# Background matmuls one at a time in a score loop: a bank held over, sums read from PSUM, work moved between VectorE and GpSimd

## The chip, the cores and the metric

The kernel runs on one core of a Trainium2 chip. A core has a matrix engine (TensorE, "PE" in the profile, with its weight loads as "PEld"), a vector engine (VectorE, "DVE"), a scalar engine for activations (ScalarE, "ACT"), a general engine (GpSimd, "POOL") and a queue engine that starts transfers (SyncE, "SP"). The metric is the device time of one execution in microseconds. Three runs before the change gave a median of 6430.78 us, from 6425.47 to 6433.72.

## The reference

The input is x of shape 8 × 128 × 36 × 36. Layer 0 normalises it in groups, applies a 1×1 convolution, and runs a convolutional attention: queries (3×3, 'SAME'), keys and values (3×3, 'VALID') of the input, softmax over 1156 key positions, then two 1×1 convolutions with a tanh between, added to x. Layer 1 takes the 1296 positions as tokens of 128 channels and applies additive attention and a gated expert layer:

```python
t = jnp.tanh(q[:, :, None, :] + k[:, None, :, :])
scores = jnp.einsum('bijd,d->bij', t, w) + bw[0]
attn = jax.nn.softmax(scores, axis=-1)
```

The scores need a tanh for each pair of tokens and each channel: 8 × 1296 × 1296 × 128 of them. The expert layer chooses 8 tokens for each of 64 experts by a softmax over the tokens, pools them, runs a small network per expert and adds its result back to the chosen tokens.

## The kernel before, in words

**The score loop.** The kernel turns the tanh sum into quotients. Each score is a sum of terms n/d, where both n and d are small matrix products over features of the keys (`kf`) and of the queries (`qf`). A *unit* is one batch, one chunk of 432 queries (three per batch) and one tile of 128 keys (ten, and a remainder of 16). A full unit has twelve *slots*, the remainder three. A slot is two halves of products: two matmuls for numerators `n` (PSUM pool `ps_n`, four banks, two taken per slot) and two for denominators `d` (pool `ps_d`, two tiles of two banks). All matmuls are fp32 and appear in the trace as two passes each. By k % 3, two slots in three contract over 32 rows ("fives"), and n of one slot and d of the slot three later stand on different rows, so they can stream together. The third is a slot of "sixes", over 64 rows.

Per slot p the program order is: pending background steps of the other engines (`take_turns`), n of slot p (`numerators`), d of slot p + 3 with its logarithm on ACT, and after every second slot an exponential that turns two logarithms into reciprocals (`denominators`, L815 and L818), the multiplies of slot p (`terms`), and then background matmuls (`matmul_turn`). Each engine takes its instructions in that order.

`terms` has two forms. For k in `DVE_PAIRS` VectorE multiplies in place in the two n banks (L836, L840) and adds them to a running sum (L837, L842), and the banks stay taken until these adds. For the others VectorE multiplies into an SBUF tile `rp` (L846, three buffers) and GpSimd adds it to its own sum (L851, L853). At the end of a unit GpSimd adds the sums (L860, L863), and ACT takes the exponential (L878).

**The background.** Everything else is cut into generators that yield between steps: `normal` (group statistics), `conv_turns` (the convolutions), `layer0`, `tokens` and `keys` for the next batch, `attend` (the weighted sum of tokens for a finished chunk) and `gating`. They stand in four lanes. A step yields whether its next one wants matmuls and how many slots it rests. A turn takes a bank with `aux(...)` from the same four of `ps_n`, so a turn's bank is one less for n; it is read by VectorE or ACT in a later step. A running account (`balance`) is debited with the columns of a turn (`behind`: the columns, at least 128, plus 20 per matmul) and credited with `PACE` per slot; a lane other than the first may begin a turn when it isn't negative.

**What the change touches.** `conv_turns` (L243) does nine taps as pairs: two matmuls into one bank, one VectorE copy or add (L258, L260), and so on. `layer0` (L329) computes, per chunk of queries, exponentials of ten score tiles, their total (L374, GpSimd), value sums in pairs of tiles (L395, L397), the total over partitions and its reciprocal on ACT (L405, L406), and the product with it (L412). `attend` (L601) does, for each of four token tiles of a chunk, eleven matmuls in two turns of six and five, with a VectorE copy (L625) and an add (L628) to join them in SBUF, then reciprocal, multiply-add and statistics (L630 to L636). `tokens` (L536) and `gate_logits` (L680) normalise tiles of 128 channels with GpSimd, about two tiles per step. Before the loop, the image of batch 1 is loaded (L917).

Of the kernel before, what the change touches and what calls it, by code (L numbers as in the profile page):

```python
# [57 lines left out]
DVE_PAIRS = (2, 5, 8, 11)  # L58
PACE = 370
# [5 lines left out]
def kernel(  # L65
# [55 lines left out]
    with ExitStack() as loop, ExitStack() as score:  # L121
# [28 lines left out]
        def aux(name):  # L150
            return ps_n.tile([128, 512], F32, tag="n", name=name)
# [73 lines left out]
        TAKE = (False, 1)  # L225
# [17 lines left out]
        def conv_turns(taps, rows, y0, x0, width, dst):  # L243
            r0, nr = rows
            for t0 in range(0, 9, 2):
                some = TAPS[t0 : t0 + 2]
                ps = aux("pc")[:, : nr * width]
                for t, (dy, dx) in enumerate(some):
                    bmm(
                        ps.rearrange("p (a b) -> p a b", b=width),  # L250
                        taps[:, (t0 + t) * C : (t0 + t + 1) * C],
                        xpad[:, y0 + dy + r0 : y0 + dy + r0 + nr, x0 + dx : x0 + dx + width],
                        start=(t == 0),
                        stop=(t == len(some) - 1),
                    )
                yield TAKE
                if t0 == 0:
                    nc.vector.tensor_copy(dst, ps)  # L258
                else:
                    nc.vector.tensor_add(dst, ps, dst)  # L260
                yield matmuls()
# [67 lines left out]
        def layer0(b):  # L329
# [33 lines left out]
            for c in range(NCH):  # L363
# [22 lines left out]
                ax = chunk_tile("ax0")  # L386
                for j0 in range(0, NDT, 2):
                    pa = aux("pa0")
                    for j in (j0, j0 + 1):
                        n = DTILES[j][1]  # L390
                        bmm(pa[:, :CH], vw[:n, j, :], ex[j][:n], start=(j == j0), stop=(j > j0))
                    yield TAKE
                    if j0 == 0:
                        total(NDT - 1)
                        nc.vector.tensor_scalar(ax, pa[:, :CH], 1.0 / D, None, ALU.mult)  # L395
                    else:
                        nc.vector.scalar_tensor_tensor(  # L397
                            ax, pa[:, :CH], 1.0 / D, ax, ALU.mult, ALU.add
                        )
                    yield matmuls()  # L400
                pt = aux("pt0")
                bmm(pt[:, :CH], ones[:DT], tot[:DT], start=True, stop=True)
                yield TAKE
                ri = chunk_tile("ri0")
                nc.scalar.activation(ri, pt[:, :CH], AF.Ln, scale=1.0 / D)  # L405
                nc.scalar.activation(ri, ri, AF.Exp, scale=-1.0)  # L406
                yield matmuls(1)
# [4 lines left out]
                nc.vector.tensor_mul(ax, ax, ri)  # L412
# [78 lines left out]
        def tokens(b):  # L491
# [44 lines left out]
            for t in range(NKT):  # L536
                n = KT[t][1]
                nc.gpsimd.tensor_scalar(
                    xh[:n, t, :C], tok[:n, t, :], mv[:n, t, 0:1], rs[:n, t : t + 1],
                    ALU.subtract, ALU.mult,  # L540
                )
                if t % 2 == 1:
                    yield step()
# [57 lines left out]
        def attend(b, c, es):  # L601
# [8 lines left out]
            for i in range(TPC):  # L610
                at = c * TPC + i
                nc.sync.dma_start(t2[:T, at, :], tokd[b][at * T : (at + 1) * T])
                sums = two.tile([T, C + 1], F32, tag="sums", name="sums")
                for some in (range(6), range(6, NKT)):
                    pa = aux("pa1")[:T, : C + 1]
                    for j in some:
                        if j < NKT - 1:
                            e, v = es[j][:, i * T : (i + 1) * T], xh[:, j, :]
                        else:
                            rows = slice(32 * i, 32 * i + REM)  # L620
                            e, v = es[j][rows, :T], xr[rows]
                        bmm(pa, e, v, start=(j == some[0]), stop=(j == some[-1]))
                    yield TAKE
                    if j < NKT - 1:
                        nc.vector.tensor_copy(sums, pa)  # L625
                        yield matmuls()
                    else:
                        nc.vector.tensor_add(sums, pa, sums)  # L628
                inv = small.tile([T, 1], F32, tag="inv", name="inv")
                nc.vector.reciprocal(inv, sums[:, C : C + 1])  # L630
                nc.vector.scalar_tensor_tensor(  # L631
                    t2[:T, at, :], sums[:, :C], inv, t2[:T, at, :], ALU.mult, ALU.add
# [16 lines left out]
        def gate_logits(b, chunks):  # L649
# [30 lines left out]
            for j, t in enumerate(tiles):  # L680
                nc.gpsimd.tensor_scalar(  # L681
# [20 lines left out]
        def gate_tokens(b):  # L702
# [41 lines left out]
            for t in range(NT):  # L744
                bmm(pp[:, :E], t2[:T, t, :], gT[t // half][:, t % half, :],
                    start=(t == 0), stop=(t == NT - 1))
            yield TAKE
# [135 lines left out]
        class Lane(deque):  # L883


            wants_matmuls, ready = True, 0

            def run(self, p):
# [4 lines left out]
                self.ready = p + rest  # L893

# [11 lines left out]
        def matmul_turn(p):  # L906
# [3 lines left out]
            for lane in lanes:  # L910
                while lane.due(p, True) and behind[0] == before:
                    if lane is not first_of_all and balance[0] < 0 or lane is gates and urgent:
                        break
                    lane.run(p)
            balance[0] = min(balance[0] - (behind[0] - before) + PACE, PACE)

        load_x(1)  # L917
# [16 lines left out]
        for p, (u, k) in enumerate(slots):  # L934
# [26 lines left out]
            matmul_turn(p)  # L961
# [187 lines left out]
```

## Time and profile before

| what | value |
|---|---|
| median of three runs | 6430.78 us |
| the profiled execution's own time | 6428.41 us |
| its span | 6426.7 us |
| granted TensorE clock, mean | 0.966 |
| first to last L815 (the score loop) | about 199 to 6244 us |
| idle of ACT before L815, waiting for PE's d | 643.3 us in 719 waits |
| idle of POOL before L853, waiting for DVE's rp | 975.3 us in 660 waits |

The page of a profile lists, in this order: the busy time of each engine; the span in 40 slices; transfers; the chain of work that ended last; and the groups of instructions, each as source line, engine, operation, tiles written and read, shapes, count, then busy time and mean in ns, then the idle time just before them and what ended it. A busy TensorE is not a TensorE at its peak, because its matmuls overlap. "n<-qf,kf" means a matmul into a tile n from tiles qf and kf. Other answers of the trace give busy times in a stretch of time, single instructions in order of time, and the waits between engines.

### The profile page before, as it was taken

The numbers are of one execution on the slowest core, as the hardware profiler recorded it, in microseconds if no ns is written. First come the engines' busy times: TensorE is split into PE (matmuls) and PEld (weight loads), VectorE is DVE, ScalarE is ACT, GpSimd is POOL, SyncE is SP. The second block draws the span as 40 slices with busy tenths as digits, with TensorE's granted clock in tenths as the row PEclk, the third lists the DMA queues.
The fourth block names the chain that finished last, engine by engine and source line by source line (L and its number), as shares of the span: only waits on it lengthen the run. The fifth ranks groups of instructions, "written<-read, shape, count | busy, mean of one in ns | idle before, by whom it ended". The sixth has DMA issues, their size and how long they took to land.

```text
span 6426.7 us, 106771 instructions
## 1 busy us (share of the span) xinstructions
PE 6054.8 (94%) x40448; PEld 2813.9 (44%) x40448; DVE 4900.4 (76%) x9315; ACT 5354.6 (83%) x5426; POOL 4798.1 (75%) x2966
## 2 busy tenths in 40 slices
PE   8999999999999999999999999999999999999986
PEld 4444444444444444444444444444444444544432
DVE  3687778877788777888788887887778877778862
ACT  1788898888888888888888888888888888989970
POOL 3677777787777877777787787778777787888870
PEclk9999999999999999999999999999999999999997
DMA  0200011000110002100111001100011000100017
GB/s 28 66 31 23 22 63 36 30 24 27 56 46 19 24 27 68 33 26 22 44 47 38 22 23 53 43 32 25 20 63 43 23 24 27 61 26 28 24 66 253
DMA packets 155284, 265.78 MB, mean 41 GB/s; under 512 B 53712, under 2 KB 79824, under 8 KB 154768
## 3 DMA queue, kind: packets, MB, share of 16 engines
q1 hardware_dynamic: 154768, 258.95, 12.5%
q8 instruction: 318, 5.21, 0.3%
q14 instruction: 198, 1.62, 0.1%
HBM read 196.81 MB, written 61.83 MB: 40 GB/s over the span
## 4 chain that ended last, share of the span: by engine, by line
PE 67%; DVE 12%; ACT 7%; issue 7%; POOL 6%; DMA 1%; SPq 0%; POOLq 0%; DVEq 0%; ACTq 0%
PE n L793 30%; PE d L793 10%; PE pc L237 7%; PE pa L237 6%; ACT lq L815 5%; DVE n L840 3%; DVE rp L846 3%; PE s L237 3%; PE pk L237 3%; PE pq L237 2%; DVE accd L842 2%; POOL accp L853 2%; DVE t L631 1%; PE n L800 1%; POOL t L681 1%
## 5 line engine op out<-in xcount | busy, mean ns | idle before, releaser
L853 POOL TENSOR_TENSOR accp<-accp,rp 128x864 f32<-128x864 f32 x1464 | 2965.2, 2025 | 1028.0 <-DVE rp L846 975.3
L793 PE MATMUL n<-qf,kf 32*128 32x432 f32 (+1 forms) x11520 | 3239.2, 579 | 93.4 <-DVE rp L846 47.0
L815 ACT ACTIVATE lq<-d 128x864 f32<-128x864 f32 x2952 | 2552.6, 882 | 690.7 <-PE d L793 643.3
L793 PE MATMUL d<-qf,kf 32*128 32x432 f32 (+1 forms) x11520 | 2876.6, 568 | 21.2 <-ACT lq L815 16.4
L846 DVE TENSOR_TENSOR rp<-n,lq 128x432 f32<-128x432 f32 x3984 | 2202.6, 600 | 623.7 <-PE d L793 399.3
L818 ACT ACTIVATE lq<-lq 128x1728 f32<-128x1728 f32 x1488 | 2429.0, 1632 | 47.1
L793 PEld LDWEIGHTS n<-qf,kf 32*128 32x128 f32 (+1 forms) x11520 | 1167.1, 187 | 1703.4 <-DVE rp L846 586.3
L793 PEld LDWEIGHTS d<-qf,kf 32*128 32x128 f32 (+1 forms) x11520 | 1038.8, 188 | 392.2 <-issue 254.1
L840 DVE TENSOR_TENSOR n<-n,lq 128x432 f32<-128x432 f32 x1440 | 811.7, 608 | 280.1 <-PE n L793 239.2
L842 DVE TENSOR_TENSOR accd<-n,accd 128x432 f32<-128x432 f32 x1440 | 867.4, 602 | 24.7
L851 POOL TENSOR_TENSOR accp<-rp 128x864 f32<-128x864 f32 x264 | 533.8, 2022 | 221.1 <-DVE rp L846 217.5
L237 PE MATMUL pa<-xh,e 128*108 128x129 f32 x1920 | 262.6, 284 | 55.6 <-DVE rp L846 34.7
L860 POOL TENSOR_TENSOR accp<-accp 128x432 f32<-128x432 f32 x264 | 290.8, 1101 | 16.2
L237 PEld LDWEIGHTS pa<-xh,e 128*108 128x108 f32 x1920 | 223.3, 175 | 179.1 <-DVE rp L846 107.4
L594 POOL TENSOR_SCALAR qf<-qf,cs_s 128x432 f32<-128x432 f32 x192 | 262.7, 1374 | 42.0 <-ACT qf L593 42.0
L863 POOL TENSOR_TENSOR accd<-accp,accd 128x432 f32<-128x432 f32 x240 | 265.6, 1107 | 28.5 <-DVE accd L842 10.4
L237 PE MATMUL s<-q,k 128*116 128x432 f32 x480 | 229.8, 570 | 3.3 <-DVE q L260 2.1
L237 PEld LDWEIGHTS pk<-xT,a_k 128*128 128x128 f32 x1408 | 172.2, 193 | 109.8 <-DVE accd L842 27.6
L374 POOL TENSOR_TENSOR tot<-tot,e 116x432 f32<-116x432 f32 x192 | 212.0, 1104 | 6.1
L835 DVE TENSOR_TENSOR accd<-n,lq 128x432 f32<-128x432 f32 x240 | 144.9, 604 | 91.6 <-PE n L793 60.5
L381 ACT ACTIVATE e<-s 116x432 f32<-116x432 f32 x240 | 125.0, 521 | 106.6 <-PE s L237 105.5
L237 PE MATMUL pk<-xT,a_k 128*128 128x128 f32 (+1 forms) x1408 | 203.2, 288 | 2.6 <-DVE accd L842 2.3
(175 smaller groups left out, 4144.4 us busy)
## 6 DMA issues: line engine op xcount, KB each, us to landing
kf<-kd SPq DMA_DIRECT2D x240, 512.0 KB
kd<-ks SPq DMA_DIRECT2D x160, 256.0 KB
w<-in_weight_dram SPq DMA_DIRECT2D x32, 1024.0 KB
x<-in_x_dram SPq DMA_DIRECT2D x8, 648.0 KB
t<-tokd SPq DMA_DIRECT2D x96, 54.0 KB
t2d<-t2T SPq DMA_DIRECT2D x24, 216.0 KB
res<-t2d SPq DMA_DIRECT2D x8, 648.0 KB
out_dram<-res SPq DMA_DIRECT2D x8, 648.0 KB
```

What stands on the lines that cost most here:

```text
L237: mm(out, lhsT, rhs, **kw)
L594: nc.gpsimd.tensor_scalar(qf[:, 1, :], qf[:, 0, :], cs_s[:, q : q + 1], None, ALU.mult)
L793: mm(outs[h][:, :CH], kf[rows[h], q, :], qf_of[b, c, q][rows[h], part, :], start=True, stop=True)
L815: nc.scalar.activation(lq[:, o : o + 2, :], d[:, :, :CH], AF.Ln)
L818: nc.scalar.activation(some, some, AF.Exp, scale=-1.0)
L840: mult(ns[h], ns[h], lq[:, o + h, :])
L842: nc.vector.tensor_add(live["d"], ns[h], live["d"])
L846: mult(rp[:, h, :], ns[h], lq[:, o + h, :])
L851: nc.gpsimd.tensor_add(live["p"], live["r"], rp)
L853: nc.gpsimd.tensor_add(live["p"], live["p"], rp)
L860: nc.gpsimd.tensor_add(s[:, 0, :], s[:, 0, :], s[:, 1, :])
L863: nc.gpsimd.tensor_add(d, s[:, 0, :], d)
```

## The change

There are five edits.

1. *Turns of one matmul.* A new yield value `HELD` marks a turn after which the bank stays open: the accumulation goes on in the lane's next turn. `conv_turns` yields after every matmul (HELD after the first of a pair), so do the value sums of `layer0`; `attend` puts all eleven matmuls in one bank, in turns of four, four and three; `gate_tokens` splits its twelve in the same way. While a lane holds, only that lane gets turns.
2. *Few turns in slots of sixes.* In a slot with k % 3 == 2 a turn needs a balance of at least `LATE` = 400. `PACE` goes from 370 to 380, and the balance may rise to twice `PACE`.
3. *Sums read from PSUM.* `attend` has no copy or add to SBUF; its reciprocal and multiply-add read the bank. In `layer0` the total and its reciprocal come before the last pair of value sums, whose sum is made in PSUM and multiplied from there; the factors 1/D are gone from both sides of the quotient.
4. *Three slots on VectorE.* `DVE_PAIRS` loses slot 11, which then goes by `rp` and GpSimd.
5. *Normalising shared.* Odd tiles of the two normalising loops go to VectorE. The load of batch 1's image before the loop is gone; `normal` makes it as for the other batches.

```diff
-DVE_PAIRS = (2, 5, 8, 11)
-PACE = 370
+DVE_PAIRS = (2, 5, 8)
+PACE, LATE = 380, 400
...
-        TAKE = (False, 1)
+        TAKE, HELD = (False, 1), (True, 1)
...
-                yield TAKE
+                    yield TAKE if t == len(some) - 1 else HELD
...
+                ri = chunk_tile("ri0")
                 for j0 in range(0, NDT, 2):
-                    pa = aux("pa0")
+                    if j0 == NDT - 2:
+                        pt = aux("pt0")
+                        bmm(pt[:, :CH], ones[:DT], tot[:DT], start=True, stop=True)
+                        yield TAKE
+                        nc.scalar.activation(ri, pt[:, :CH], AF.Ln)
+                        nc.scalar.activation(ri, ri, AF.Exp, scale=-1.0)
+                        yield matmuls()
+                    pa = aux("pa0")[:, :CH]
                     for j in (j0, j0 + 1):
                         n = DTILES[j][1]
-                        bmm(pa[:, :CH], vw[:n, j, :], ex[j][:n], start=(j == j0), stop=(j > j0))
-                    yield TAKE
+                        bmm(pa, vw[:n, j, :], ex[j][:n], start=(j == j0), stop=(j > j0))
+                        yield TAKE if j > j0 else HELD
                     if j0 == 0:
                         total(NDT - 1)
-                        nc.vector.tensor_scalar(ax, pa[:, :CH], 1.0 / D, None, ALU.mult)
+                        nc.vector.tensor_copy(ax, pa)
+                    elif j0 < NDT - 2:
+                        nc.vector.tensor_add(ax, pa, ax)
                     else:
-                        nc.vector.scalar_tensor_tensor(
-                            ax, pa[:, :CH], 1.0 / D, ax, ALU.mult, ALU.add
-                        )
+                        nc.vector.tensor_add(pa, pa, ax)
+                        nc.vector.tensor_mul(ax, pa, ri)
                     yield matmuls()
...
-                nc.gpsimd.tensor_scalar(
+                (nc.gpsimd, nc.vector)[t % 2].tensor_scalar(
...
-                sums = two.tile([T, C + 1], F32, tag="sums", name="sums")
-                for some in (range(6), range(6, NKT)):
-                    pa = aux("pa1")[:T, : C + 1]
...
+                pa = aux("pa1")[:T, : C + 1]
+                for j in range(NKT):
...
+                    bmm(pa, e, v, start=(j == 0), stop=(j == NKT - 1))
+                    if j in (3, 7):
+                        yield HELD
+                yield TAKE
                 inv = small.tile([T, 1], F32, tag="inv", name="inv")
-                nc.vector.reciprocal(inv, sums[:, C : C + 1])
+                nc.vector.reciprocal(inv, pa[:, C : C + 1])
                 nc.vector.scalar_tensor_tensor(
-                    t2[:T, at, :], sums[:, :C], inv, t2[:T, at, :], ALU.mult, ALU.add
+                    t2[:T, at, :], pa[:, :C], inv, t2[:T, at, :], ALU.mult, ALU.add
                 )
...
+                if t in (3, 7):
+                    yield HELD
...
-        def matmul_turn(p):
+        def matmul_turn(p, k):
             before = behind[0]
-            for lane in lanes:
+            least = LATE if k % 3 == 2 else 0
+            for lane in [lane for lane in lanes if lane.holds] or lanes:
                 while lane.due(p, True) and behind[0] == before:
-                    if lane is not first_of_all and balance[0] < 0 or lane is gates and urgent:
+                    if lane is not first_of_all and balance[0] < least or lane is gates and urgent:
                         break
                     lane.run(p)
-            balance[0] = min(balance[0] - (behind[0] - before) + PACE, PACE)
-
-        load_x(1)
+            balance[0] = min(balance[0] - (behind[0] - before) + PACE, 2 * PACE)
```

## The prediction

> **What bounds the kernel now.** I read the page's busy shares first, then the chain that ended last and the costliest groups.
>
> ```profile
> span 6426.7 us, 106771 instructions
> PE 6054.8 (94%) x40448; PEld 2813.9 (44%) x40448; DVE 4900.4 (76%) x9315; ACT 5354.6 (83%) x5426; POOL 4798.1 (75%) x2966
> PE 67%; DVE 12%; ACT 7%; issue 7%; POOL 6%; DMA 1%; SPq 0%; POOLq 0%; DVEq 0%; ACTq 0%
> ...
> L853 POOL TENSOR_TENSOR accp<-accp,rp 128x864 f32<-128x864 f32 x1464 | 2965.2, 2025 | 1028.0 <-DVE rp L846 975.3
> ...
> L815 ACT ACTIVATE lq<-d 128x864 f32<-128x864 f32 x2952 | 2552.6, 882 | 690.7 <-PE d L793 643.3
> L846 DVE TENSOR_TENSOR rp<-n,lq 128x432 f32<-128x432 f32 x3984 | 2202.6, 600 | 623.7 <-PE d L793 399.3
> ```
>
> No engine is full: ACT waits 643 us for denominators from PE, POOL 975 us for products from DVE. TensorE carries the chain but its busy share includes pipeline latency. A unit (12 slots of one key tile) is the right ruler, so I next read the busy times of six single units of batches 4, 5 and 7. The columns are busy us of PE, PEld, DVE, ACT, POOL, then the clock.
>
> ```profile
> 3318.62:3347.20 28.58, 24.87 (x111) 10.92 (x110) 22.73 (x41) 20.42 (x21) 26.09 (x23) 0.82 0.03 5
> 3428.19:3450.39 22.20, 21.90 (x110) 9.76 (x106) 19.57 (x37) 20.31 (x20) 16.58 (x10) 1.00 0.22 78
> 3522.54:3548.09 25.55, 22.77 (x157) 12.96 (x155) 24.30 (x49) 20.29 (x21) 16.34 (x9) 1.00 0.09 25
> 3593.98:3620.07 26.09, 26.06 (x178) 10.11 (x175) 17.98 (x33) 24.49 (x30) 24.07 (x17) 1.00 0.07 21
> 3911.01:3940.48 29.47, 24.43 (x112) 11.22 (x115) 21.35 (x40) 20.31 (x20) 25.85 (x23) 0.77 0.06 19
> 6181.65:6201.59 19.94, 19.23 (x98) 7.68 (x96) 16.73 (x31) 19.75 (x20) 16.33 (x10) 1.00 0.00 1
> ```
>
> The last has no background: 19.94 us, ACT 19.75 of them. That is the floor. The others: gate normalising (28.58, POOL 26.09); a convolution (22.20); attention sums (25.55, DVE 24.30); scores s (26.09, ACT 24.49 and POOL 24.07); token normalising (29.47, POOL 25.85). So what ends a unit differs by its background. Loop time from first to last Ln is 6045 us; less 24 remainder units at about 7 us, 240 full units average 24.5.
>
> Two waits matter. The time-ordered view shows one bank wait: the second n matmul starts only when the first in-place add of the slot before is done (1014.62 + 0.62 = 1015.24), since the transposes hold one of four banks, and the next Ln starts after 1.27 us idle. And it shows VectorE against POOL:
>
> ```profile
> 1013.32 0.59 PE L241 MATMUL tp<-ident,t 108*128 108x108 f32 x4
> 1013.60 1.11 DVE L840 TENSOR_TENSOR n<-n,lq 128x432 f32<-128x432 f32 x2
> ...
> 1014.62 1.24 DVE L842 TENSOR_TENSOR accd<-n,accd 128x432 f32<-128x432 f32 x2
> ...
> 1015.27 0.62 PE L793 MATMUL n<-qf,kf 32*128 32x432 f32 x1 [0.44 <-DVE accd L842]
> ...
> 1016.35 0.89 ACT L815 ACTIVATE lq<-d 128x864 f32<-128x864 f32 x1 [1.27 <-PE d L793]
> ```
>
> ```profile
> 4086.65 3.70 DVE L291 SCALAR_TENSOR_TENSOR dev<-dev,gn_mv 128x1 f32<-128x1 f32 x1
> ```
>
> This DVE instruction has one element per lane and lasts 3.70 us, until POOL's run of operations (four L681, one L853: 4085.23 to 4090.34) is over.
>
> **What the skill says.** "SBUF — State Buffer", Who interferes with whom: VectorE and GpSimd share a port pair under an exclusive lock; a VectorE instruction with two SBUF inputs, or a tensor_scalar in the two-port mode, is shut out for whole GpSimd instructions, one with at most one SBUF input is not. The trace agrees: L631 (two SBUF inputs) has median 674 ns, 350 to 1841; L846 (one from PSUM) is steady at 600. "VectorE: DVE Perf Modes", Mode 2×_2P — use both read ports for one tensor: an fp32 tensor_scalar from SBUF to SBUF takes both ports. L213, such a one of 11 or 12 elements, lasts 0.158 to 1.37 us, which agrees. "TensorE: Matmul & The Clock Gate", What's actually happening: the clock drops when PE has been idle; the two normalising units show 0.82 and 0.77.
>
> **The change part by part**, against the profiled execution (6428.4 us, span 6426.7).
>
> *Sums read PSUM.* Per token tile (96 in all) one copy L625 (0.288) and one add L628 (0.292) go, and L631 loses its second SBUF input: 0.915 mean toward the 0.350 minimum. That is 0.58 + 0.565 = 1.14 us of DVE. An attention unit does about 3 tiles; its L631 are the bad ones (1.664 mean in the unit above), so DVE loses 3 × (0.58 + 1.31) = 5.7 us, and 1.2 more from the slot below: 24.3 falls to 17.4. VectorE no longer bounds it. What is late next is PE: I take the 25.5 down by 1.2 only, because of the held bank (below). Range 0 to 3. There are 44 × 2 passes per chunk against 56 or so in a unit, 1.55 units per chunk, 4.6 per batch: −5.5 us a batch. Dividing by D moved from L395/L397 to nowhere, and L412 (0.816) becomes a PSUM multiply of 0.604 (as L846): 24 × 0.21 = 5 us, off the path. The pt turn goes ahead of the last pa0 turn: its two ACT passes (0.516 + 0.563) now hide under pa0 matmuls. Nothing counted.
>
> *Three slots on VectorE.* Slot 11 moves: per unit DVE loses two adds, 2 × 0.602 = 1.2 us (289 us in all; the multiplies stay), POOL gains one L853, 2.025 us (486 us in all). POOL at 4798 goes to 5284, less the normalising below (11 tiles a batch, about 0.79 each, 8 batches, −70): 5214. Convolution units end on PE with DVE 19.6 close: I give them −0.2 each, 8 a batch: −1.6. Score and query-block units have ACT 24.5 and POOL 24.1; POOL becomes 26.1 of 26.1, the first to fill: +0.3 each (0 to +1), 7 a batch: +2.
>
> *One-matmul turns, bank held.* PE's work is the same: the same matmuls, same banks' sums. A 2-matmul turn put 1.44 us (four passes of 432 columns, which follow each other at 0.36) between a slot and the next; now 0.72. Denominators come more evenly, but a bank is held over most slots instead of some 40% of them (370/904). With it held, the second n waits for the slot before: after a PSUM-multiply slot that is about hidden by n, d and one turn; after an in-place slot, the add ends some 2.7 us after n began (1.0 + 1.1 + 0.6), PE alone needs 1.7, so 1.0 us is exposed unless a turn fills 0.72. Behind that n on PE stand the next d and so ACT's next Ln. Slots of sixes need a balance of 400, so with 380 per slot and 452 per turn a convolution skips about one in six slots, always a six, half of them while held; attention turns (4 × 149 = 596) skip nearly every six while held. Cost: about 0.4 × 1.0 per in-place slot in convolutions, 0.75 × 1.0 in attention, times three. Against it stand the lumps: the ACT idle of 643 us. I take both as cancelling in convolutions and the attention cost as already in the −1.2 above.
>
> *Normalising shared.* Five of eleven L538 and six of twelve L681 per batch move to DVE: POOL loses 11 × 0.79 = 8.7 us in two units with POOL near 26 of 29, where DVE then idles on POOL (4.40 us before one L846), PE behind it. POOL gains 2.0 per unit. On DVE each costs some 0.2 us alone (a 128-element bn_stats takes 0.27) but may wait for POOL, up to the 3.70 above; behind it on DVE stand the slot's multiplies, so the banks, so PE. Net per unit between −5 and +3; I take −2.5, two a batch: −5.
>
> *The rest.* Group load x[1] goes from the start into the loop, where batches 2 to 7 already have it four slots ahead of use: 0. PACE 380 for 370 finishes the background 2.7% sooner: 0 at constant work. In the tail the last chunk's three waiting tiles save 0.58 each and four L681 in a row (3.12) are halved: −3.
>
> Sum: −5.5 − 1.6 + 2 − 5 = −10.1 a batch; times 7.5 (the first batch's preparation lies before the loop, the last has no successor) = −76, with the tail −79. 6428 − 79 = 6349, so 6350 in the runs, whose median 6430.8 lies 2 us over the profiled one.
>
> **Rivals.** (A) Held banks and POOL win: slower. From the point where every in-place slot exposes its 1.0 us while held in 60% of cases, 240 × 3 × 0.6 = +430 us less the lumps' relief of about half the 643 us: +110, with POOL's +2 unchanged and my gains halved (−40): 6500. For it: 535 PE weight loads already wait on L842 for 248 us. Against: many fall in slots that PE fills anyway. Chance 0.27. (B) Nothing moves: PE passes plus their gaps fill about 92% of a unit (22.2 of the convolution's), so smoothing has nothing to win and DVE's relief is slack: 6425. Chance 0.07. (C) Large gain: lumps were the cause of ACT's idling and half of the 643 us returns, plus the sum above less overlaps (−79 + 20): −380, 6050; half as strong, 6240. For: units run at 19.94 when undisturbed. Against: convolution units are only 2.3 over it with ACT's own background work inside. Chance 0.16 for below 6270. My forecast 0.50.
>
> **Numbers.** A measurement tells about 0.2% (13 us) from no change. Faster 0.68 (0.50 + 0.16 + edge of B), same 0.05, slower 0.27. Range 6220 to 6500 holds most of the forecast, B and A's nearer half; the forecast's own is 6290 to 6410.
>
> **What would show it.** Right: attention units near 24 us with L631 at 0.4; L625 and L628 gone; L853 near 1700 instructions; POOL above 80%; normalising units under 27. Wrong: n waiting on L842 well over 248 us with ACT idle above 643, or DVE tensor_scalars of several us.

## The result, and the profile after

The changed kernel took 6549.68 us (median of four runs, 6539.88 to 6552.72) against 6432.25 us for the kernel before on the same chip: a ratio of 1.0182, 95% interval 1.0164 to 1.0199. It is slower by 117 us, and lies 50 us above the upper end of the predicted range.

The page of the changed kernel, with the lines that answer to those shown of before (line numbers are one lower there: L852 was L853, L814 was L815, L845 was L846, L841 was L842):

```profile
span 6549.1 us, 106863 instructions
PE 6230.2 (95%) x40448; PEld 2792.7 (43%) x40448; DVE 4594.4 (70%) x8731; ACT 5372.1 (82%) x5426; POOL 5206.4 (79%) x3118
PE 63%; POOL 15%; issue 8%; DVE 7%; ACT 6%; DMA 1%; SPq 0%; POOLq 0%; ACTq 0%; DVEq 0%
L852 POOL TENSOR_TENSOR accp<-accp,rp 128x864 f32<-128x864 f32 x1704 | 3448.8, 2024 | 961.3 <-DVE rp L845 884.1
L845 DVE TENSOR_TENSOR rp<-n,lq 128x432 f32<-128x432 f32 x4464 | 2488.6, 601 | 1231.8 <-PE d L792 659.3
L814 ACT ACTIVATE lq<-d 128x864 f32<-128x864 f32 x2952 | 2570.7, 883 | 797.6 <-PE d L792 721.0
```

The moves happened as planned: VectorE fell by 306 us (4900.4 to 4594.4), GpSimd rose by 408 (4798.1 to 5206.4). But GpSimd's share of the chain that ended last went from 6% to 15%, and ACT now waits 721 us for denominators, not 643. The list of waits shows what changed. Its columns are the waiting engine and tile, what it waited for, us in total, times, and the longest. First after, then before:

```profile
PEld n L792 <- DVE rp L845: 793.7, 1207, 3.6
PEld pa L238 <- issue: 214.3, 385, 1.2
PEld pc L238 <- issue: 198.6, 389, 1.2
PEld n L792 <- DVE accd L841: 153.7, 269, 2.3
DVE rp L845 <- POOL accp L850: 144.8, 86, 3.2
DVE rp L845 <- POOL accp L852: 76.7, 54, 3.5
```

```profile
PEld n L793 <- DVE accd L842: 248.3, 535, 3.3
DVE rp L846 <- POOL accp L851: 78.1, 32, 8.7
PEld pc L237 <- issue: 66.4, 371, 0.6
PEld pa L237 <- issue: 46.9, 272, 0.2
```

VectorE's products now wait 222 us for GpSimd to free an `rp` tile, 78 before. And the weight loads of background turns stand 413 us at "issue" (waiting for nothing that the profile shows), 113 before. The "issue" time by itself is no measure of a loss: it falls to 244 us in the run below with turns of two, for 32 us of time, and is still 403 us in the run with a fourth buffer, which is 130 us faster. The wait that the slower rival was built on, n for the in-place add, fell from 248 to 154, about as the number of those adds did (L841 x960, from x1440).

Single units of batch 4 show where the time is (columns as before: busy us of PE, PEld, DVE, ACT and POOL with their counts, clock, transfers). The first is unit 0 of chunk 0, then come unit 6 of chunk 0 (a convolution) and units 0 and 1 of chunk 1 (the last does attention sums):

```profile
3308.87:3338.20 29.33, 25.03 (x109) 12.36 (x110) 15.62 (x29) 20.73 (x21) 24.17 (x14) 0.83 0.07 22
3471.02:3495.08 24.06, 23.93 (x123) 9.04 (x119) 18.89 (x36) 20.33 (x20) 18.34 (x10) 1.00 0.06 22
3568.46:3597.24 28.78, 27.31 (x128) 11.81 (x126) 17.57 (x33) 21.06 (x22) 21.88 (x13) 0.88 0.07 22
3597.24:3622.03 24.79, 24.79 (x165) 13.74 (x163) 18.37 (x41) 20.54 (x21) 18.36 (x10) 1.00 0.09 27
```

The first units of chunks took 23.45 and 23.15 us before; now they take 29.33 and 28.78 at a lower clock. Over all 24 chunks the first units, each from its first Ln to the next unit's, take 650.2 us, 557.5 before: 93 of the 125 us that the score loop lost. The attention unit is hardly shorter than its 25.55, although VectorE is down from 24.30 to 18.37. Inside the third of these units, in order of time (start, duration, engine, what; in brackets the idle time before it and what ended it):

```profile
3578.14 1.12 POOL L862 TENSOR_TENSOR accd<-accp,accd 128x432 f32<-128x432 f32 x1
...
3579.21 1.38 POOL L596 TENSOR_SCALAR qf<-qf,cs_s 128x432 f32<-128x432 f32 x1
...
3579.95 1.65 ACT L814 ACTIVATE lq<-d 128x864 f32<-128x864 f32 x2
...
3580.54 2.04 POOL L850 TENSOR_TENSOR accp<-rp 128x864 f32<-128x864 f32 x1
...
3582.62 1.12 DVE L845 TENSOR_TENSOR rp<-n,lq 128x432 f32<-128x432 f32 x2 [2.58 <-POOL accp L850]
...
3583.28 0.96 PE L792 MATMUL n<-qf,kf 64*128 64x432 f32 x1 [1.32 <-DVE rp L845]
...
3586.44 0.89 ACT L814 ACTIVATE lq<-d 128x864 f32<-128x864 f32 x1 [3.16 <-PE d L792]
```

The same core in a stretch just after the stall, with its clock:

```profile
3586.00:3590.00 4.00, 4.00 (x13) 1.39 (x13) 1.49 (x4) 1.07 (x2) 0.77 (x1) 0.50 0.00 0
```

The old unit's slots 9, 10 and 11 all went to GpSimd, its two sums and a feature product follow, so the first add of the new unit starts late. Slots 0 and 1 of the new unit need `rp` tiles too, five slots in a row, and slot 0's tile is only freed by slot 1's add (L850). VectorE's next product has no `rp` tile until that add ends (2.58 us), the banks stay full, PE starts no matmul for some 1.3 us, its granted clock then is 0.50, and ACT is idle for 3.16 us.

### The profile page after: what moved, and what is told of

It reads as the page before. It is cut to its first block, busy times and chain, and to the rows that moved or that the text cites. A ratio compares the mean times of both kernels' runs of the same rounds, so it can differ in the third digit from the quotient of the medians.

```text
span 6549.1 us, 106863 instructions
## 1 busy us (share of the span) xinstructions
PE 6230.2 (95%) x40448; PEld 2792.7 (43%) x40448; DVE 4594.4 (70%) x8731; ACT 5372.1 (82%) x5426; POOL 5206.4 (79%) x3118
## 4 chain that ended last, share of the span: by engine, by line
PE 63%; POOL 15%; issue 8%; DVE 7%; ACT 6%; DMA 1%; SPq 0%; POOLq 0%; ACTq 0%; DVEq 0%
PE n L792 29%; PE d L792 9%; PE pa L238 7%; PE pc L238 7%; POOL accp L852 7%; ACT lq L814 4%; PE s L238 3%; DVE n L839 2%; DVE rp L845 2%; POOL qf L596 2%; POOL accp L850 2%; PE pk L238 2%; DVE accd L841 1%; POOL accp L859 1%; PE d L799 1%
## 5 line engine op out<-in xcount | busy, mean ns | idle before, releaser
L852 POOL TENSOR_TENSOR accp<-accp,rp 128x864 f32<-128x864 f32 x1704 | 3448.8, 2024 | 961.3 <-DVE rp L845 884.1
L792 PE MATMUL n<-qf,kf 32*128 32x432 f32 (+1 forms) x11520 | 3330.7, 583 | 126.3 <-DVE rp L845 93.4
L845 DVE TENSOR_TENSOR rp<-n,lq 128x432 f32<-128x432 f32 x4464 | 2488.6, 601 | 1231.8 <-PE d L792 659.3
L814 ACT ACTIVATE lq<-d 128x864 f32<-128x864 f32 x2952 | 2570.7, 883 | 797.6 <-PE d L792 721.0
L792 PE MATMUL d<-qf,kf 32*128 32x432 f32 (+1 forms) x11520 | 2957.3, 572 | 44.6 <-ACT lq L814 40.7
L839 DVE TENSOR_TENSOR n<-n,lq 128x432 f32<-128x432 f32 x960 | 545.3, 609 | 226.4 <-PE n L792 206.9
L841 DVE TENSOR_TENSOR accd<-n,accd 128x432 f32<-128x432 f32 x960 | 577.7, 602 | 16.4
L850 POOL TENSOR_TENSOR accp<-rp 128x864 f32<-128x864 f32 x264 | 533.6, 2021 | 31.7 <-DVE rp L845 31.4
L238 PEld LDWEIGHTS pa<-xh,e 128*108 128x108 f32 x1920 | 238.8, 182 | 190.8 <-issue 124.5
L238 PE MATMUL pa<-xh,e 128*108 128x129 f32 x1920 | 298.3, 296 | 9.2 <-DVE accd L841 4.6
L238 PE MATMUL pa<-e,vw 116*128 116x432 f32 x480 | 231.2, 571 | 1.3 <-DVE accd L841 0.5
```

The source lines that it names most:

```text
L238: mm(out, lhsT, rhs, **kw)
L792: mm(outs[h][:, :CH], kf[rows[h], q, :], qf_of[b, c, q][rows[h], part, :], start=True, stop=True)
L814: nc.scalar.activation(lq[:, o : o + 2, :], d[:, :, :CH], AF.Ln)
L839: mult(ns[h], ns[h], lq[:, o + h, :])
L841: nc.vector.tensor_add(live["d"], ns[h], live["d"])
L845: mult(rp[:, h, :], ns[h], lq[:, o + h, :])
```

## The experiments

### Slot 11 back on VectorE, longer turns, GpSimd's normalising, the old account

Four runs undo one part each in the changed kernel.

*Slot 11.*

```diff
-DVE_PAIRS = (2, 5, 8)
+DVE_PAIRS = (2, 5, 8, 11)
```

> The kernel after, with slot 11 back on VectorE (four slots in place). POOL theory (GpSimd, with three rp slots in a row at the end of a unit and the sums behind them, makes VectorE wait for rp buffers; those waits are 222 us of the L850 and L852 rows after, 78 and a little before): most of them go and the first units of a chunk fall from 29 toward 24, so 6450 to 6480. Switch theory (each extra change of PE between slot products and a background turn costs about 0.24 us, 520 more of them): slot 11 has no part in it, 6535 to 6555.

Measured: 6454.81 us, 1.0037 of the kernel before (1.0024 to 1.0050). Putting it back alone returns 95 of the 117 us. In the score loop of the two traces 87 of 92 us lie in the first units of chunks (563.1 us, from 650.2). Some of it comes by way of the clock: its mean is 0.964 in the changed kernel and 0.975 here, which is 74 us less of TensorE's time lost to a lower clock (6549 × 0.036 less 6453 × 0.025; an estimate, and the most that the clock can have given). The products' wait for GpSimd is down to this:

```profile
DVE rp L845 <- POOL accp L850: 31.3, 20, 2.4
```

*Turns of two matmuls in convolutions and value sums.*

```diff
-                    yield TAKE if t == len(some) - 1 else HELD
+                yield TAKE
...
-                        yield TAKE if j > j0 else HELD
+                    yield TAKE
```

> The kernel after, with the convolutions' and value sums' matmuls again in turns of two, so without a bank held between their turns (attention and pooling keep theirs). Switch theory: some 51 turns a batch go, 408 in all, at 0.24 us: -98, so 6450, and the small gaps of PE return to those of before. POOL theory: these waits stay, 6530 to 6560.

Measured: 6518.01 us, 1.0135 (1.0118 to 1.0152): 32 us less than the changed kernel, between the two expectations. With slot 11 on VectorE in both kernels the same step is worth 68 us (6454.81 above, 6387.02 below).

*All normalising on GpSimd.*

```diff
-(nc.gpsimd, nc.vector)[t % 2].tensor_scalar(
+nc.gpsimd.tensor_scalar(
```

> The kernel after, with both normalising loops on GpSimd alone. Port theory (VectorE's share waits for GpSimd; 40 xh tiles at 0.878 us and 48 t tiles at 0.540): VectorE gets back 60 us, some of it on the path, -20: 6530. POOL theory: GpSimd gets 70 us more in its two fullest units of a batch: 6560 to 6600.

Measured: 6591.89 us, 1.0252 (1.0237 to 1.0267). Sharing it is worth 42 us, as the second theory had it.

*The old account* (`PACE = 370`, `LATE = 0`, balance up to `PACE`; held turns stay).

> The kernel after, with the account of before: 370 per slot, at most 370, and no rule for slots of sixes. Held-bank theory (a skipped slot of sixes leaves a held bank's wait exposed): a turn now stands there as often as elsewhere, -30 to -60: 6490 to 6520. Switch theory: the number of turns is the same, 6540 to 6560. If turns in slots of sixes were what hurts, 6570 to 6600.

Measured: 6587.43 us, 1.0243 (1.0228 to 1.0258). The new account is worth 38 us in this kernel. That is the range of the last theory, turns in slots of sixes; but the credit and its limit were undone together with the rule for these slots, so the rule alone isn't shown.

### Both undone, and a step further

*Slot 11 on VectorE and turns of two.*

> The kernel after, with slot 11 back on VectorE and the convolutions' and value sums' matmuls in turns of two again. If the two causes add (95 and 32 us so far): 6550 - 127 = 6423, level with before. If the pairs save more once GpSimd no longer disturbs them (switch theory, 98 us): 6360.

Measured: 6387.02 us, 0.9931 (0.9914 to 0.9947). The two undone together return 163 us, more than their 95 + 32. Why they don't add was not tested.

*The same, attention in one bank in turns of six and five, pooling in one turn.*

```diff
-                    if j in (3, 7):
+                    if j == 5:
...
-                if t in (3, 7):
-                    yield HELD
```

> As a_both, and also attention in one bank in turns of six and five, and pooling in one turn: some 14 turns fewer a batch. Switch theory at 0.24 us each: 27 us below a_both; at the 0.08 that the pairs alone showed: 9 below. Held-bank theory (finer turns feed ScalarE more evenly): 10 to 30 above a_both.

Measured: 6378.10 us, 0.9914 (0.9900 to 0.9929). Its interval overlaps with that of the run above; the 9 us that the attention and pooling turns gave aren't told apart from nothing.

### The two suspects alone, on the kernel before

*Three slots on VectorE, nothing else.*

> The kernel before, with slot 11 on GpSimd and nothing else. POOL theory: the same cost as in the kernel after, some 95 us: 6525, with VectorE's waits for L851 and L853 above 150 us in place of 80. If it hurts only beside a held bank: 6430 to 6450.

Measured: 6471.89 us, 1.0061 (1.0046 to 1.0076), 39 us slower, between the two expectations. The products' waits for GpSimd rose from 81 to 279 us (L851 and L853), far more than the time did. In the traces the first units of chunks take 53 us more than before (610.5 and 557.5) and unit 3 of chunk 0, where gate tiles are normalised, 23 us more (249.2 and 226.2); all other units together take 35 us less.

*Convolutions and value sums in held turns of one, nothing else* (the old account).

> The kernel before, with one-matmul turns and the bank held in the convolutions and value sums alone (51 turns a batch more, account as before). Switch theory: between 32 us (as the pairs gave) and 98 (at 0.24 each): 6460 to 6530, with PE's gaps around background turns up. Lump theory (shorter turns feed ScalarE more evenly): 6350 to 6400.

Measured: 6499.89 us, 1.0108 (1.0092 to 1.0127), 67 us slower. A convolution has 648 turns instead of 360 in the whole program (72 chunks, nine for five), the value sums 240 instead of 120: 408 more. The first batch's 51 of them run before the score loop, where no slots stand between turns; in the loop it is 357.

### A fourth buffer

```diff
-        kstp = pool("kstp", 3, score, "right")
+        kstp = pool("kstp", 2, score, "right")
...
-        rpp = pool("rpp", 3, score, "right")
+        rpp = pool("rpp", 4, score, "right")
```

> The kernel after the change with four rp buffers in place of three (and two buffers in place of three for another tile of the key features, to make room). Theory 1, depth: slot 11 through GpSimd costs 95 us because three rp slots follow each other (9, 10, 11) and then the unit's sums, so that VectorE's next product waits for a free rp (228 us of such waits in all, 86 before); one more buffer takes most of these waits and with them most of the 95: 6460 to 6480. Theory 2, rate: GpSimd is simply full in those units, a buffer only moves the wait by a slot or two: 6530 to 6550, the waits of rp for GpSimd above 180 us. Theory 3: these waits are not the cause, the cost is that VectorE's products of slot 11 keep the second half's banks longer; then also 6550, but with the waits of rp for GpSimd well under 100 us.

Measured: 6419.13 us, 0.998 (0.997 to 0.999), 130 us less than the changed kernel and faster than the kernel before. "Depth" is shown and "rate" falls: GpSimd is as busy as in the changed kernel (5206.5 us), yet the products' waits for it are 50 us, from 222. The two units that took 29.33 and 28.78:

```profile
3254.03:3277.21 23.18, 21.81 (x110) 9.99 (x110) 15.46 (x29) 20.51 (x22) 22.63 (x14) 1.00 0.09 28
3504.55:3527.95 23.40, 23.25 (x128) 10.67 (x126) 17.32 (x32) 20.95 (x21) 21.91 (x13) 1.00 0.09 28
```

```profile
DVE rp L845 <- POOL accp L852: 37.4, 28, 2.2
DVE rp L845 <- POOL accp L850: 12.5, 15, 1.1
```

The same place as in the timeline above; the product waits 0.28 us, for PE, and the next L814 starts 3.23 us after the pair of L814 at 3515.97 (6.49 us in the changed kernel, from 3579.95 to 3586.44):

```profile
3515.33 1.36 POOL L596 TENSOR_SCALAR qf<-qf,cs_s 128x432 f32<-128x432 f32 x1
...
3516.34 1.12 DVE L845 TENSOR_TENSOR rp<-n,lq 128x432 f32<-128x432 f32 x2 [0.28 <-PE d L792]
...
3516.66 2.02 POOL L850 TENSOR_TENSOR accp<-rp 128x864 f32<-128x864 f32 x1
...
3519.20 0.87 ACT L814 ACTIVATE lq<-d 128x864 f32<-128x864 f32 x1
```

The 130 us exceed slot 11's 95: the buffer does something else as well. In the score loops of the traces (132 us apart) the first units give 83 us, and unit 3 of chunk 0, with the last of the gate normalising, 27. The other half of the edit, two `kstp` buffers for three, was not tried alone.

### Number of turns, or the bank held over

*The bank held one slot longer, nothing split* (the balance may rise to twice the credit).

```diff
-        TAKE = (False, 1)
+        TAKE, LONG = (False, 1), (False, 2)
...
-                yield TAKE
+                yield LONG
...
-            balance[0] = min(balance[0] - (behind[0] - before) + PACE, PACE)
+            balance[0] = min(balance[0] - (behind[0] - before) + PACE, 2 * PACE)
```

> The kernel before, turns of two matmuls as they are, but each turn of a convolution and of the value sums keeps its bank one slot longer (its copy or add rests two slots), and the balance may rise to twice the credit so that the work isn't late for that. Nothing is split. Rival theory, held bank: it was the bank held over that cost the 67 us of the split turns; then this one, which holds banks in about as many slots, is 6470 to 6500, with the waits of n for the in-place add well over 248 us. Theory, turn count: the 67 us are the gaps around 400 additional turns, and a bank held longer costs under 15 us: 6420 to 6445.

Measured: 6683.64 us, 1.0395 (1.0379 to 1.0410), 255 us slower. My expectation was far off. Of the 480 turns that hold a bank one slot longer 420 stand in the score loop (the first batch's 60 run before it), so it is 0.61 us for each, with what the higher limit of the balance did in it. Of the rival's signs, ACT's wait for d went from 643 to 829 us, but n for the in-place add only from 248 to 269. A convolution unit, first of the kernel before, then of this run:

```profile
3405.91:3428.19 22.28, 22.26 (x122) 9.77 (x114) 19.68 (x37) 20.12 (x20) 16.37 (x9) 1.00 0.08 24
```

```profile
3553.72:3580.01 26.29, 25.88 (x117) 10.44 (x117) 18.99 (x36) 20.32 (x21) 16.38 (x9) 1.00 0.07 21
```

PE's busy time grew by 3.6 us, with no more matmuls in the records (117 for 122). A place in that unit suggests a reason: of a slot's two n matmuls one starts beside nothing, the other only after VectorE's product, so n and d no longer stream side by side as they do when both banks are free.

```profile
3559.56 1.57 PE L793 MATMUL n<-qf,kf 32*128 32x432 f32 x3
...
3560.50 0.18 PEld L793 LDWEIGHTS n<-qf,kf 32*128 32x128 f32 x1 [0.76 <-DVE rp L846]
```

This reading is argued from single places, and the edit also moves the turns to every second slot. So in this form a bank held longer costs much; whether that is what split turns pay is the next run's question.

*As many turns as in the split run, no bank held:* every tap and every value sum starts and stops in a turn of its own, and VectorE adds it.

```diff
-            for t0 in range(0, 9, 2):
-                some = TAPS[t0 : t0 + 2]
+            for t0 in range(9):
+                some = TAPS[t0 : t0 + 1]
...
-                for j0 in range(0, NDT, 2):
+                for j0 in range(NDT):
```

> The kernel before with every tap of the convolutions and every value sum in a turn of its own, started and stopped in one matmul and copied or added by VectorE after it, as after every pair before: as many turns as with the split and held turns (6500), no bank held over, 408 more adds on VectorE (about 0.6 us each, in units where VectorE is busy 19.6 of 22 us). Theory, turn count: the gaps around 400 more turns cost some 70 us, whatever the bank does, less half of that for smaller lumps; with the adds 6470 to 6520. Theory, held bank: without holding, single turns cost little and take lumps away: 6400 to 6440.

Measured: 6489.58 us, 1.0092 (1.0077 to 1.0107), 59 us slower with no bank held over. A loss of nearly the split run's 67 us is thus there without the hold; the hold's own part is 8 us plus whatever the 408 more adds cost this run. The convolution unit shown above, in the split run and in this one, speaks against a large price of the adds: VectorE is 1.5 us busier here, and the unit is no longer.

```profile
3460.29:3483.08 22.79, 22.76 (x113) 9.05 (x106) 19.51 (x37) 20.22 (x19) 16.35 (x9) 1.00 0.07 24
```

```profile
3439.80:3462.48 22.68, 22.66 (x114) 8.93 (x106) 20.99 (x40) 20.23 (x20) 16.36 (x9) 1.00 0.08 24
```

The price of a turn can be read off PE. In the changed kernel, a turn of one matmul (two passes of 374 columns):

```profile
3580.13 0.91 PE L238 MATMUL pc<-xpad,wv_t 128*128 128x374 f32 x2
...
3580.97 0.99 PE L792 MATMUL n<-qf,kf 64*128 64x432 f32 x2
```

and in the kernel before, a turn of two (four passes):

```profile
3511.01 1.56 PE L237 MATMUL pc<-xpad,wv_t 128*128 128x374 f32 x4
...
3512.50 1.00 PE L793 MATMUL n<-qf,kf 64*128 64x432 f32 x4
```

From the turn's first matmul to the slot's next it is 0.84 us for one and 1.49 for two. Two turns of one take 2 × 0.84 − 1.49 = 0.19 us more than one of two. Over the whole traces the medians of such turns are 0.84 and 1.48, and at 432 columns 0.92 and 1.65, so it is about the same everywhere. The 357 additional turns in the score loop make 68 us (357 × 0.19, an estimate), against 67 and 59 measured.

*Fewer turns: nine taps in three turns of three.*

> The kernel before with the nine taps of a convolution in three turns of three instead of five turns of two and one; all else as before. Theory, turn count: 144 turns fewer at 0.24 us each, 35 us less: 6390 to 6405. Rival, lumps: a turn of three puts 2.16 us between a slot and the next and ACT waits longer for its denominators: 6445 to 6480, and the waits of ACT for d above 643 us.

Measured: 6458.22 us, 1.0045 (1.0028 to 1.0062), 30 us slower, where the turn count alone would give 24 us less (126 of the 144 turns stand in the loop, at 0.19 us). ACT waits 35 us longer for its denominators (643.3 before):

```profile
ACT lq L815 <- PE d L793: 678.1, 706, 9.1
```

That is what the rival expected: lumps count too, then, from three matmuls on, and turns of two are the best of the three sizes on this kernel.

*The same in the version that won so far.*

> The best kernel so far (four slots on VectorE, turns of two taps, attention in one bank in turns of six and five, pooling in one turn, the new account and the shared normalising) with convolutions in three turns of three. Theory, turn count: 35 us less than its 6378: 6345. Rival, lumps: 6390 to 6420. With the new account, whose turns stay out of slots of sixes when the balance is low, long turns could fit less well than in the kernel before; then about 6375.

Measured: 6382.33 us, 0.9923 (0.9908 to 0.9938): no different from turns of two (6378.10). With the new account long turns are kept out of the slots of sixes; that this is why they don't hurt there was not tested.

### The sums from PSUM alone, and with the buffer

*On the kernel before, only attention's part of edit 3, turns of six and five as before.*

```diff
-                sums = two.tile([T, C + 1], F32, tag="sums", name="sums")
-                for some in (range(6), range(6, NKT)):
-                    pa = aux("pa1")[:T, : C + 1]
...
+                pa = aux("pa1")[:T, : C + 1]
+                for j in range(NKT):
...
+                    if j == 5:
+                        yield HELD
```

> The kernel before with edit 3's attention part alone: eleven matmuls in one bank, in turns of six and five as before, the bank held between them; reciprocal and multiply-add read PSUM; copy and add to SBUF gone. All else as before, the old account too. Forecast's step: 5.5 us a batch, 41 in all: 6390. Rival, held bank: 96 turns held over one or more slots at the 0.53 us of the run with longer-held banks take back 50 or more, and it is 6430 to 6450.

Measured: 6437.12 us, 1.0009 (1.0001 to 1.0018): no gain. Two attention units, and the two instructions that now read the bank:

```profile
3274.29:3299.21 24.92, 24.69 (x157) 13.66 (x152) 19.73 (x42) 20.43 (x20) 16.36 (x9) 1.00 0.09 26
3527.50:3552.18 24.68, 24.62 (x162) 13.92 (x161) 18.93 (x43) 20.43 (x20) 16.36 (x9) 1.00 0.08 26
```

```profile
L626 DVE SCALAR_TENSOR_TENSOR t<-pa,inv,t 108x128 f32<-108x128 f32 x96 | 33.7, 351 | 28.3 <-DMA t<-tokd 24.6 <-DVE inv L625 0.5
...
L625 DVE RECIPROCAL inv<-pa 108x1 f32<-108x1 f32 x96 | 16.1, 168 | 68.5 <-PE pa L237 68.5
```

VectorE was relieved (24.30 to 18.93 us in the second), but the unit ends on PE, busy in 24.6 of 24.7 us. And the reciprocal now waits 68.5 us for the last matmul of its bank; copy and add waited 7.4 + 17.4 for PE before. The time lies in the rival's range: that the bank held between the two turns took a gain back was not excluded.

*The same with four `rp` buffers.*

> The run before this with four rp buffers (two instead of three for a tile of key features, to make room). If the fourth buffer helps only where slot 11 goes through GpSimd: the same as that run within 15 us. If GpSimd's runs of other work (normalising, sums of exponentials) stall VectorE's products by themselves: 30 to 60 us below it.

Measured: 6383.68 us, 0.9926 (0.9910 to 0.9943), 53 us below, though all four slots are on VectorE. So three buffers were already too few before the change; the products' waits for GpSimd fall from 73.3 to 24.4 us here, and the gain lies where GpSimd has other work. In batch 4, the first seven units of the first chunk, with gate normalising, went from 160.5 to 155.3 us (from one first Ln to another), units 4 to 6 of the third chunk with the remainder, with token normalising, from 93.6 to 88.5; the stretch between these two took 442.4 and 442.2.

*The same with three slots on VectorE.*

> The same with four rp buffers and slot 11 through GpSimd. Theory, depth: three rp slots in a row with four buffers cost nothing, and VectorE is relieved of 1.2 us a unit: 0 to 30 us below the run with four slots and four buffers. Theory, rate: GpSimd at 80% still stalls the units with other GpSimd work: 20 to 60 us above it.

Measured: 6375.90 us, 0.9916 (0.9902 to 0.9931): with four buffers slot 11 through GpSimd costs nothing.

### All gains together

*The version with turns of two and attention in six and five, with four buffers, slot 11 on GpSimd, then on VectorE.*

> The changed kernel with turns of two taps and two value sums, attention in one bank in turns of six and five, pooling in one turn, three slots on VectorE and four rp buffers (two instead of three for a tile of key features). If the causes are the gaps of more turns and the rp wait, and they add: 6419 (four buffers) less 32 to 60 for the longer turns: 6360 to 6385, or, with the interaction that was seen between slot 11 and the turns, down to 6335. If shared normalising and the fourth buffer pay for the same stall (GpSimd's runs of other work) they don't add: about 6375, as without them.

> The same with slot 11 back on VectorE (four slots). The same without the fourth buffer was 6378. If shared normalising already took the stall away that the fourth buffer takes, 6370 to 6378; if not, 6325 to 6345. Against the run with three slots: 0 to 15 us above it, as on the kernel before.

Measured: 6316.70 us, 0.9821 (0.9807 to 0.9836), and 6350.73 us, 0.9870 (0.9853 to 0.9887). Both are faster than anything above, the first faster than it was expected to be, the second between its two ranges. The first is 114 us faster than the kernel before and 233 faster than the change as it was made, and moving slot 11 now gains 34 us where it had cost 95. Its page:

```profile
span 6314.9 us, 106639 instructions
PE 6049.1 (96%) x40448; PEld 2769.9 (44%) x40448; DVE 4597.6 (73%) x8731; ACT 5346.7 (85%) x5426; POOL 5207.7 (82%) x3118
PE 63%; DVE 11%; POOL 10%; issue 8%; ACT 7%; DMA 1%; SPq 0%; POOLq 0%; DVEq 0%; ACTq 0%
```

```profile
ACT lq L812 <- PE d L790: 503.3, 585, 3.9
DVE rp L843 <- POOL accp L850: 39.6, 31, 2.1
```

VectorE and GpSimd are as busy as in the changed kernel, to 4 us; what changed is how long they and ACT wait. ACT's idle time for d is 503 us, from 721.

## Why the prediction was wrong

The forecast was 6350, faster at 0.68. Put together from the runs, the 117 us are about: sums from PSUM +6, sharing −42, new account −38, 408 split turns +67, 112 more turns in attention and pooling +21 (at 0.19, an estimate; the run that undid them measured 9), slot 11 +95. That is +109. That it comes so near is in part luck: slot 11 and the split turns are 95 and 32 when undone in the changed kernel, 39 and 67 when made alone, and 163 when undone together, so the sum is a guide, not a proof.

- **One-matmul turns, "PE's work is the same", cancelling in convolutions: this step failed.** The sum had 0; alone they cost 67 us. I counted passes at 0.36 us, 0.72 for a turn of one and 1.44 for a turn of two, and gave entering and leaving a turn no price; the traces show 0.92 and 1.65. The Trainium skill, "TensorEngine Tiling (Array Packing)", Key Properties, says that changing the tiling mode drains TensorE; a turn uses all 128 rows between matmuls on 32 or 64, so each turn changes it twice. The page has no price, and no run here separates the drain from the rest of the 0.19 us, but it is a reason to have asked. The number of turns accounts for it: the run without held banks lost 59 us, and 357 turns at 0.19 make 68. A small part of the held bank, 8 us and what the adds cost, is not excluded.
- **Three slots on VectorE, +2 and −1.6 a batch: this step failed too.** It was sized as a rate: 2.0 us more on GpSimd in a unit of 22 to 26 us. What bound was depth: three `rp` tiles for three `rp` slots at the end of a unit, then the unit's sums, and two more such slots at the start of the next. It cost 39 us on the kernel before and 95 on the changed one. The prediction never asked how many products could wait for GpSimd, though the waits of the kernel before had 78 us of exactly that.
- **Sums from PSUM, −5.5 a batch: right in its instructions, wrong in its worth.** The price of a tile was 1.14 us; the rows give (27.7 + 28.0 + 87.9 − 33.7)/96 = 1.14. L631 fell from 0.915 to 0.351. Of the 1.2 us a unit nearly nothing came: alone the edit gave +6 us in all. "What is late next is PE" was right, but the 1.2 us behind it was not.
- **Normalising shared, −2.5 a unit, −37 in all: right.** It measured 42. The VectorE form takes 0.54 us on average for gate tiles and 0.88 for token tiles, not 0.2; single ones last 2.07 or 1.84, until a GpSimd add that began before them is over, and others 0.33. The Trainium skill, "SBUF — State Buffer", Who interferes with whom, says that a VectorE instruction in a two-port mode and GpSimd shut each other out for whole instructions. The trace agrees beside GpSimd's tensor_tensor, not beside its tensor_scalar: of these VectorE instructions 25 began inside a GpSimd tensor_scalar with at least 0.3 us of it to come, and they took 0.33 to 0.44 us.
- **The new account at 0: it was a gain.** Undoing it cost 38 us, in a kernel that has held turns; what it does for unheld ones was not run.
- **Rival A, slower, 6500: its side was right, its mechanism not.** Its sign was n waiting on the in-place add well over 248 us; that fell to 154. ACT's idle time did rise, to 721. Its 1.0 us for an exposed held bank is of the right order in the run with longer holds (0.61 for each turn), but the split turns' holds cost little beside their number. That its 6500 came nearer to 6550 than the forecast did is luck.
- Of what was to be seen: L625 and L628 are gone, L852 has 1704 instructions, GpSimd is at 79% (80 expected); the attention unit shown is at 24.79, not 24; of the normalising units of batch 4 the gate's two took 26.76 and 23.94 us, the tokens' 26.95 (under 27 expected).
- Two readings in the prediction are off and carry nothing: the 0.158 us of L213 belong to a form with fewer than 11 elements (with 11 or 12 the shortest is 0.164), and a bn_stats (L635) takes 0.29 us, not 0.27.

Open: why slot 11 costs 39 us on the kernel before, 95 on the changed one and 131 (6518.01 less 6387.02) with turns of two (the first units lose 53, 87 and 100 us of it, in the traces; what the other units do with the relief of VectorE differs); and how much of the 130 us is due to two `kstp` buffers for three.

## What to carry to other kernels

Before work is moved to an engine that takes its input through a ring of buffers, count the longest run of such inputs in program order across the ends of units too, and add what else stands in that engine's queue: an engine at 80% stalled its producer for 222 us at three buffers and for 50 at four. Price a split by its entries and exits, not by its columns: here 0.19 us for each turn more on PE, so that on the kernel before smoothing paid only down to two matmuls. And undo two suspects together as well as singly, since what they cost need not add (95 and 32 singly, 163 together): the change that looked worst (slot 11) is a gain of 34 us in the kernel with the fourth buffer and turns of two.

## What the runs showed of the hardware

- A background turn in the score loop took 0.84 us for two passes of 374 columns and 1.49 us for four, from its first matmul to the next slot's, so that two turns of one took 0.19 us more than one of two.
- A stall of VectorE on GpSimd of 2.58 us, in which PE started no matmul for some 1.3 us, was followed by a granted clock of 0.50 (3586 to 3590 us), and two passes took 1.09 us (3587.88) where they took 0.63 before it (3579.19). ACT stood for 3.16 us, and from Ln to Ln the place took 3.26 us more than in the run with a fourth buffer (6.49 and 3.23).
- Banks held one slot longer, with nothing split and a higher limit of the balance, cost 0.61 us for each turn of the loop that held one, and PE's busy time in a convolution unit rose by 3.6 us without more matmuls.
- A VectorE tensor_scalar of a normalised tile (128 columns) in the changed kernel waited out a GpSimd tensor_tensor (up to 2.08 us) but ran beside a GpSimd tensor_scalar in 0.33 to 0.44 us.
